# A two-layer graph, state-space and mixture kernel: earlier lists and counts, four dense steps moved into the features, the last listed sums moved into the second mixture, and the last loads split in halves

## The chip, the cores and the metric

The kernel runs on one core of one Trainium2 chip, as one program with one launch. The core has five engines that run side by side, each through its own list of instructions in order: TensorE (PE in the profile; its weight loads are PEld), VectorE (DVE), ScalarE (ACT), GpSimd (POOL) and SyncE (SP, which only issues transfers). Transfers are carried out by 16 DMA engines. The metric is the device time of one execution in microseconds, the median of several executions. No clock of the host comes into it.

## The reference

There are 4096 tokens with 256 features, and one fixed 4096x4096 matrix `adj` (about 9 nonzero entries in a row, each row divided by its number of entries). Two layers follow each other, and each adds the result of a graph block and then that of a mixture of experts:

```python
# layer 0
h = layernorm(relu(adj @ layernorm(x) @ gcn_w + gcn_b))
xz = h @ w_in                       # 256 -> 2 x 512
u  = silu(causal_conv4(xz[:, :512])); z = xz[:, 512:]
dt, B, C = projections of u         # softplus for dt
for t: state = exp(dt[t] * A) * state + dt[t] * B[t] * u[t]     # 512 x 16
       ys[t] = state @ C[t]
x1 = x + ((ys + u * D_skip) * silu(z)) @ w_out
x2 = x1 + sum over 2 of 8 experts: weight * (gelu(n @ W1) @ W2),   n = layernorm(x1)
# layer 1
f   = tanh(relu(adj)**2), of each row the 700 largest kept
h2  = tanh(layernorm(x2) @ W_proj + b_proj)
x3  = x2 + relu(f @ (h2 @ W_gcn) + b_gcn)
out = x3 + sum over 2 of 6 experts (three layers each), weights by softmax
```

A row of `adj` has far fewer than 700 positive entries, so the 700 largest are all of them. The kernel counts the positive entries of each row, and only if a count is over 700 does it run a slow second way at its end.

## The kernel before, in words

**Tiling.** Tokens go in 8 chunks of 512 (`NC`, `CW`), each of four tiles of 128. Everything is computed in float32. The span has seven stages, in this order.

1. *Start.* The graph product of layer 0 for chunk c is the generator `propagation(c)`: two halves of 256 columns, each of 32 pieces, a piece being two matrix products; every four pieces need one 512 KB tile `at` of the transposed matrix, from a ring of three buffers. With `count=True` VectorE also adds up, for each `at` tile, which entries are positive (`cnt`, lines 864 and 866; each reads the tile, so the tile's buffer is free again only after TensorE and VectorE have both read it). At the end of a half the counts are summed over partitions by TensorE and their maximum goes to `cmax`. Chunk 0 is counted here. Beside it, `lists.pair` (lines 543 to 640) makes *lists*: for chunks 2, 4 and 6 (`LISTED`) the nonzero entries of a row are found by VectorE as up to 24 positions and values. Two of the six pairs of tiles are made in this stage (`EARLY_PAIRS`, 12 steps of the generator each), the other four in stage 3. The lists of stage 1 take their buffers from the tile name `hc`.
2. *Scans.* `Front(c)` prepares a chunk (its pieces of work are placed at steps by `PLAN` and `EARLY`), then 32 steps a chunk do two scans on VectorE (line 1377), a product by C (1387), the input product on GpSimd (1354) and sums on TensorE (1404). The last work of `Front(0)` on VectorE ahead of the first scan is `do_soft` (lines 1081 to 1089), in four parts.
3. *First mixture* of layer 0, with `expert_tiles`.
4. *Features* (`features`): per chunk the mixture's result is loaded (`yg`) and combined, normalised, turned by TensorE, projected (`project`), and multiplied by W_gcn (`weigh`) into `gn`, which also goes to the DRAM tensor `gnd`.
5. *Dense steps.* For chunks 0, 1, 3, 5 and 7 the product f @ gn is done in 16 steps each, 80 in all (`seq`, counted by k): `fetch(k)` loads 512 KB of the matrix, `source(k)` turns it into f by three ScalarE activations and, except in chunk 0, adds to the chunk's count on VectorE; `product(k)` is 8 matrix products. `finish(c)` adds bias and residual. Sources run `LEAD` = 3 steps ahead, loads `AHEAD` = 2 more; three f tiles are made ahead of the features already. In the same loop the listed chunks are done by gathers (`Listed`): a *slot* is one gather of 128 rows of `gnd` by GpSimd (line 1726) into one of 12 row buffers, and one or two multiply-adds of 128x256 into x3 on VectorE (1742), 216 slots and 288 sums in all. `taken.upto(int(PACE * (k - 2)))` fixes after which step which slot is summed; a buffer that is summed is at once refilled. Four row buffers are tiles of their own (`ring`), four lie in x3 of chunk 7 and four in x3 of chunk 6 until those are written. `ROUTES` names the step at which the routing of a finished chunk begins (about 13 pieces, one a step), `TABLES` the step at which the tables of the second mixture begin.
6. *Second mixture* (`tiles1`), first the 23 tiles of chunks 0 to 4, then the 15 of chunks 5 to 7. Per tile: two gathers by GpSimd (`xk`, line 495), four turns, a copy by VectorE (`xkT`, 737), three layers, a bias add on VectorE (`yk`, 702) and two scatters by GpSimd (504). `also(n)` adds a little other work after each tile: in the first 23 the routing of chunks 7, 6, 5, later the outputs of chunks 0 to 4.
7. *End.* For chunks 5 to 7 both rows of each token are loaded, weighted, added to x3 and stored (`to_out`, `combine`): chunk 5 in whole loads of 512 KB, chunk 6 in halves, chunk 7 whole; all on the SP queue, with three `yg` buffers.

**What sets the order.** In stages 1, 2, 4 and 5 the order of each compute engine is the order in which the program text issues the work; in stages 4 and 5 that holds for SP too. Elsewhere a scheduler places instructions by its own estimate. Either way the order is fixed when the program is built: on the chip each engine takes its list in turn and waits at whatever is not ready.

Of the kernel before, what the change touches and what calls it, by code (L numbers as in the profile page):

```python
# [10 lines left out]
F32 = mybir.dt.float32  # L11
# [25 lines left out]
PACE = 2.85  # L37
ROUTES = {17: 0, 29: 2, 33: 1, 49: 3, 55: 4}
TABLES = 69
# [7 lines left out]
def kernel(ctx: ExitStack, tc: tile.TileContext, out: bass.AP, **a):  # L47
# [735 lines left out]
    with ExitStack() as s1:  # L783
# [70 lines left out]
        def propagation(c, count=False):  # L854


            halves = psts[c] = []
            for r0 in range(c * CW, c * CW + CW, HW):
                pt = ps_pt.tile([P, DB, HW], F32, name="pt", tag="pt")
                for j4 in range(NT // 4):  # L860
                    at = ats.pop(0) if ats else adjacency(r0, j4)
                    if count and j4 == 0:
                        cnt = w2p.tile([P, 4, HW], BF16, name="cnt0", tag="db")
                        nc.vector.tensor_scalar(cnt, at, 0.0, None, ALU.is_gt)
                    elif count:
                        nc.vector.scalar_tensor_tensor(cnt, at, 0.0, cnt, ALU.is_gt, ALU.add)
                    for jj in range(4):
                        j = 4 * j4 + jj
                        for k in range(DB):

                            nc.tensor.matmul(  # L871
                                pt[:, k, :], xl[:, j, k * P:(k + 1) * P], at[:, jj, :],
                                start=(j == 0 and k == 0), stop=(j == NT - 1 and k == DB - 1),
                            )
                        yield
# [3 lines left out]
                if count:  # L879
                    pc = ps_y.tile([P, CW], F32, name="psy", tag="psy")  # L880
                    for jj in range(4):
                        nc.tensor.matmul(
                            pc[:1, :HW], ones[:, :1], cnt[:, jj, :], start=(jj == 0), stop=(jj == 3)
                        )
                    h = (r0 // HW) % 2
                    nc.vector.tensor_reduce(chalf[:, h:h + 1], pc[:1, :HW], AX.X, ALU.max)
                    if h == 1:
# [527 lines left out]
        with tc.manual_schedule(engines={  # L1415
# [71 lines left out]
            for _ in range(EARLY_LISTS - NT // 4):  # L1487
                next(made)
            prop, left = propagation(1), 2 * NT + 2 - late
            for i in range(9, STEPS):  # L1490
                fr.at(i, Front.EARLY)
                fr.at(i)
                if i == 11:
                    for _ in made:
                        pass
# [3 lines left out]
            advance(left)  # L1499
            steps, tails, kept, gated, summed, owed = [], [], {}, [], 0, 0  # L1500
# [86 lines left out]
    with ExitStack() as s2:  # L1587
# [109 lines left out]
        ring += [x3[:, NT - TPC + t, :] for t in range(TPC)]  # L1697
# [7 lines left out]
        for t in ring + early_ring:  # L1705
            nc.gpsimd.memset(t, 0.0)
# [3 lines left out]
        class Listed:  # L1710
# [3 lines left out]
            def __init__(self):  # L1714
                self.slots = [(q, s) for q in range(lists.n) for s in range(PAIR)]
                self.free, self.at, self.next, self.done = early_ring + ring, {}, 0, 0
                self.last = len(self.slots) - TPC // 2 * PAIR - 12

            def fetch(self):
                if self.next >= self.last:  # L1720
                    self.free = [f for f in self.free if any(f is r for r in ring)]
# [10 lines left out]
            def upto(self, n):  # L1732
                while self.done < min(n, len(self.slots)):
# [20 lines left out]
                    self.fetch()  # L1754

# [52 lines left out]
        def features():  # L1808
# [6 lines left out]
            for c in range(1, NC):  # L1815
                if c + 1 < NC:
                    fs[c + 1].sums()
                fs[c].turn()
                fs[c - 1].weigh()
                if c + 1 < NC:  # L1820
# [21 lines left out]
        def source(k):  # L1842
# [6 lines left out]
            if c == 0:  # L1849
# [47 lines left out]
        with tc.manual_schedule(engines={  # L1897
# [8 lines left out]
            features()  # L1906
            taken.fetch()
            for k, (c, j2) in enumerate(seq):
                if k == TABLES:
# [16 lines left out]
                if k >= TABLES:  # L1926
                    next(table, None)
                taken.upto(int(PACE * (k - 2)))
                product(k, pf)
                if j2 == H2 - 1:  # L1930
                    ended = (c, pf, total(c) if c else None)
            finish(*ended)
        assert not routes and taken.done == len(taken.slots)
# [35 lines left out]
    with ExitStack() as s4:  # L1969
# [10 lines left out]
        def routing():  # L1980
            for b in range(NC - SPLIT - 1, -1, -1):
# [11 lines left out]
        def also(n):  # L1993
            if n == few[0]:
# [12 lines left out]
        for b in range(NC - SPLIT):  # L2007
            stores.append(to_out(dp1[1], b, op[0], 1 + b % 2))
# [165 lines left out]
```

## Time and profile before

| | us |
|---|---|
| median of 7 runs | 2304.73 |
| lowest and highest | 2299.45, 2309.87 |
| the profiled execution | 2303.46 |
| its span, first to last instruction | 2301.6 |
| TensorE busy in the span | 2087.7 (91%) |
| VectorE busy | 1812.5 (79%) |
| GpSimd busy | 1393.2 (61%) |
| ScalarE busy | 1195.8 (52%) |

Stage limits in the span, from the first instructions of each: start 0 to 158, scans to 1253, first mixture to 1570, features to 1672, dense steps to 2015, second mixture to 2275, end to 2301.6.

How to read it: times are microseconds from the first instruction of the span. "L1742" is line 1742 of the kernel before. A timeline line gives start, length, engine, line, operation, written tile `<-` read tiles, the number of instructions merged into it, and in brackets the idle time of that engine just before it and what ended it. In a table of stretches each engine has its busy time and, in brackets, its instructions; then the granted TensorE clock (1.00 is full speed), the busy share of the DMA engines, and what they moved.

### The profile page before, as it was taken

The page shows a single profiled execution, that of the slowest core. Times are in us where ns is not written, and L with a number is a line of the kernel's source. Part 1 is how long each engine was busy: PE and PEld are TensorE (multiplying, and loading weights), DVE is VectorE, ACT ScalarE, POOL GpSimd, SP SyncE. Part 2 cuts the span into 40 slices and gives each one's busy share as a digit, 9 for nine tenths or more (in the row PEclk, how much of TensorE's full clock was granted, in tenths as well). Part 3 has the DMA queues.
Part 4 walks back from the last instruction along what each step waited for, and adds up shares of the span by engine and source line. Part 5 has one row for each costly group of instructions (what it writes and reads, how often), then busy time and mean ns, then how long its engine had stood idle before and what let it go on. Part 6 is the DMA issues. An engine that isn't in the chain of part 4 may idle for free. (4 is left out here: it accounts for less than half of the span.)

```text
span 2301.6 us, 28092 instructions
## 1 busy us (share of the span) xinstructions
PE 2087.7 (91%) x8235; PEld 1494.1 (65%) x8235; DVE 1812.5 (79%) x3207; ACT 1195.8 (52%) x2064; POOL 1393.2 (61%) x1056
## 2 busy tenths in 40 slices
PE   7898999999999999989799799995899989899994
PEld 6665564666656566655466588783588778678773
DVE  6959999999999999999998889214448999954242
ACT  4145746566574656657675222422488677533221
POOL 1027778777777878777764445442067777856651
PEclk9999999999999999999899799997899999999997
DMA  9549999998999999899885899863265555477794
GB/s 292 175 147 260 235 274 243 257 264 229 279 243 273 247 245 270 238 270 269 236 280 175 282 329 354 254 204 126 101 190 180 177 155 175 143 236 217 241 327 157
DMA packets 302677, 532.29 MB, mean 231 GB/s; under 512 B 31323, under 2 KB 170575, under 8 KB 301616
## 3 DMA queue, kind: packets, MB, share of 16 engines
q1 hardware_dynamic: 244720, 416.84, 56.5%
q0 software_dynamic: 57792, 113.54, 22.1%
q8 instruction: 69, 1.13, 0.2%
q14 instruction: 96, 0.79, 0.1%
HBM read 434.34 MB, written 49.02 MB: 210 GB/s over the span
## 5 line engine op out<-in xcount | busy, mean ns | idle before, releaser
L1354 POOL TENSOR_TENSOR db<-du,bb 128x1024 f32<-128x1024 f32 x256 | 607.0, 2371 | 312.4 <-DVE hc L1387 74.9
L1377 DVE TENSOR_TENSOR_SCAN db<-da,state,db 128x512 f32<-128x512 f32 x512 | 627.2, 1265 | 20.4 <-ACT da L1370 18.1
L871 PE MATMUL pt<-at,gn 128*128 128x256 f32 x2048 | 479.2, 387 | 17.5 <-ACT gn L129 9.8
L871 PEld LDWEIGHTS pt<-at,gn 128*128 128x128 f32 x2048 | 396.9, 195 | 138.9 <-issue 62.7
L1370 ACT ACTIVATE da<-dt,negA 128x512 f32<-128x512 f32 x512 | 346.1, 688 | 245.4 <-DVE db L1377 235.7
L1387 DVE TENSOR_TENSOR hc<-db,cb 128x1024 f32<-128x1024 f32 x256 | 327.4, 1279 | 17.8 <-issue 0.4
L1404 PE MATMUL psy<-hc,ident 128*128 128x512 f32 x560 | 291.4, 614 | 1.9 <-DMA hc<-hc 1.9
L1864 PE MATMUL pf<-gn,f 128*128 128x256 f32 x1280 | 289.0, 387 | 0.0
L1864 PEld LDWEIGHTS pf<-gn,f 128*128 128x128 f32 x1280 | 247.1, 194 | 37.0 <-issue 3.3
L712 PE MATMUL ps_h<-xkT,wk 128*128 128x256 f32 x864 | 213.8, 390 | 13.1 <-DVE xkT L737 10.1
L697 PE MATMUL ps_y<-wk,hk 128*128 128x256 f32 x864 | 214.1, 383 | 0.2
L702 DVE TENSOR_TENSOR yk<-ps_y,bk 128x512 f32<-128x512 f32 x73 | 50.2, 688 | 204.2 <-PE ps_y L697 171.8
L1391 POOL DMA_DIRECT2D hc<-hc x232 | 201.9, 870 | 0.2
L712 PEld LDWEIGHTS ps_h<-xkT,wk 128*128 128x128 f32 x864 | 159.5, 193 | 49.0 <-DVE xkT L737 14.9
L1726 POOL DMA_INDIRECT x<-gnd,ls_idx x128 | 149.2, 1166 | 62.3 <-DMA gnd<-gn 21.7
L697 PEld LDWEIGHTS ps_y<-wk,hk 128*128 128x128 f32 x864 | 161.6, 192 | 21.8 <-ACT hk L716 1.4
L1404 PEld LDWEIGHTS psy<-hc,ident 128*128 128x128 f32 x560 | 105.2, 194 | 81.8 <-issue 59.6
L999 PE MATMUL ps_xz<-hT,w_in 128*128 128x512 f32 x256 | 117.0, 600 | 14.1 <-ACT hT L983 7.4
L1726 POOL DMA_INDIRECT ring<-gnd,ls_idx x88 | 110.1, 1251 | 31.3 <-issue 11.6
L716 ACT ACTIVATE hk<-ps_h,d0r_b 128x256 f32<-128x256 f32 x104 | 49.0, 473 | 137.5 <-PE ps_h L712 137.5
L1016 PE MATMUL ps_xz<-xc,dK 128*128 128x512 f32 x256 | 114.8, 592 | 0.0
L1846 ACT ACTIVATE f<-at 128x1024 f32<-128x1024 f32 x80 | 84.4, 1055 | 48.8 <-PE pf L1864 39.0
(398 smaller groups left out, 2998.5 us busy)
## 6 DMA issues: line engine op xcount, KB each, us to landing
at<-in_adjT_dram SPq DMA_DIRECT2D x208, 512.0 KB, 4.8
bb<-bcd SPq DMA_DIRECT2D x128, 512.0 KB, 5.3
cb<-bcd SPq DMA_DIRECT2D x128, 512.0 KB, 5.2
hc<-hc POOLq DMA_DIRECT2D x232, 256.0 KB, 5.5
wk<-in_L_ffn_W_dram SPq DMA_DIRECT2D x70, 512.0 KB, 6.2
wk<-in_L_ffn_expert_w_dram SPq DMA_DIRECT2D x114, 256.0 KB, 4.0
ls_at<-in_adj_dram SPq DMA_DIRECT2D x32, 512.0 KB, 8.5
hc<-in_adj_dram SPq DMA_DIRECT2D x16, 512.0 KB, 5.1
```

The costliest lines, as they stand in the source:

```text
L697: nc.tensor.matmul(ps[:, j, :], hT[:, m, j * P:(j + 1) * P], w[:, m, :], start=(m == 0), stop=(m == kb_out - 1),)
L712: nc.tensor.matmul(ps[:, j, :], w[:, d, m * P:(m + 1) * P], xT[:, d, :], start=(d == 0), stop=(d == DB - 1),)
L871: nc.tensor.matmul(pt[:, k, :], xl[:, j, k * P:(k + 1) * P], at[:, jj, :], start=(j == 0 and k == 0), stop=(j == NT - 1 and k == DB - 1),)
L999: nc.tensor.matmul(ps, w_in[:, k, m * P:(m + 1) * P], self.hT[:, k, :], start=(k == 0), stop=(k == DB - 1),)
L1354: nc.gpsimd.tensor_tensor(self.db, self.f.du[self.half][:, self.mi:self.mi + 1, :].to_broadcast([P, 2, CW]), self.bb, ALU.mult,)
L1370: nc.scalar.activation(da, self.f.dt[self.half][:, self.mi, :], AF.Exp, scale=negA[:, self.m, n:n + 1])
L1377: nc.vector.tensor_tensor_scan(self.db[:, j, :], da, self.db[:, j, :], state[:, self.m, n:n + 1], ALU.mult, ALU.add,)
L1387: nc.vector.tensor_tensor(self.hc, self.db, self.cb, ALU.mult)
L1391: nc.gpsimd.dma_start(self.hc[:, 0, :], self.hc[:, 1, :], accum_op=ALU.add)
L1404: nc.tensor.matmul(f.psy[m], ident, self.hc[:, j, :], start=False, stop=(self.g == GS - 1 and j == last),)
L1726: nc.gpsimd.indirect_dma_start(out=to[:, :], out_offset=None, in_=gnd[:, :], in_offset=bass.IndirectOffsetOnAxis(ap=lists.idx[:, q, s:s + ...
L1864: nc.tensor.matmul(pf[:, t, :], f[:, jj, t * P:(t + 1) * P], gn[:, j, :], start=(j == 0 and t % 2 == 0), stop=(j == NT - 1 and t % 2 == 1),)
```

## The change

- **Start.** The 12 list steps stay in the loop of chunk 0 only as far as 8; the other 4 of the first pair and all 12 of the second no longer stand ahead of `Front(0)`'s VectorE work, but are spread behind it, from step 11 on. Chunk 1 is now counted in `propagation(1, True)` as well (16 `cnt` instructions, the buffers taken from the names `du` and `dt`, one sum of both halves in the bank of `pt`), and no longer in the dense loop.
- **Features.** The steps k = 0 to 3 (`FIRST1`) of the dense product are done inside `features`, one in each of the rounds c = 2 to 5, ahead of the turn; the source and load that go with a step follow `weigh`. The dense loop begins at k = 4, and its slots go by `2.8 * (k - 6)`. `ROUTES` and `TABLES` move with it; the last tables come two pieces a step.
- **Listed sums.** Twelve slots are left when the dense loop ends. They use only the four buffers of `ring` (from the fourth last step on, `narrow`), and `also` takes two slots after each tile (`SPARE`). The late routing takes chunk 5, then 7, then 6, since chunk 6 is the listed one that is finished last.
- **End.** All twelve half loads of chunks 5 to 7 (256 KB each) are issued at once, one of each pair on SP and one on ScalarE's queue, into twelve buffers of the tile pool; sums and stores go by halves, the stores alternately on both queues.

```diff
-PACE = 2.85
-ROUTES = {17: 0, 29: 2, 33: 1, 49: 3, 55: 4}
-TABLES = 69
+PACE = 2.8
+SPARE = 2
+FIRST1 = 4
+ROUTES = {17: 0, 33: 2, 35: 1, 49: 3, 59: 4}
+TABLES = 72
...
                     if count and j4 == 0:
-                        cnt = w2p.tile([P, 4, HW], BF16, name="cnt0", tag="db")
+                        h = (r0 // HW) % 2
+                        tag = {"tag": "db"} if c == 0 else {"tag": ("du", "dt")[h], "bufs": 3}
+                        cnt = w2p.tile([P, 4, HW], BF16, name="cnt0", **tag)
+                        cnts.append(cnt)
...
-            for _ in range(EARLY_LISTS - NT // 4):
-                next(made)
-            prop, left = propagation(1), 2 * NT + 2 - late
+            prop, left = propagation(1, True), 2 * NT + 2 - late
             for i in range(9, STEPS):
                 fr.at(i, Front.EARLY)
                 fr.at(i)
                 if i == 11:
-                    for _ in made:
-                        pass
+                    next(made)
+                elif i > 11:
+                    for _ in range(2 if i < 14 else 1):
+                        next(made, None)
...
-                self.free, self.at, self.next, self.done = early_ring + ring, {}, 0, 0
+                self.free, self.at, self.next, self.done = early_ring + late_ring + ring, {}, 0, 0
+                self.kept = ring + late_ring
...
+            def narrow(self):
+                self.kept = ring
+
+            def lent(self):
+                return [g for g, f in self.at.items() if any(f is r for r in late_ring)]
...
             for c in range(1, NC):
                 if c + 1 < NC:
                     fs[c + 1].sums()
+                k = c - 2
+                if 0 <= k < FIRST1:
+                    product(k, pf)
                 fs[c].turn()
                 fs[c - 1].weigh()
+                if 0 <= k < FIRST1:
+                    source(k + LEAD)
+                    fetch(k + LEAD + AHEAD)
                 if c + 1 < NC:
                     fs[c + 1].norm()
                 fs[c].project()
...
-            if c == 0:
+            if c < 2:
                 pass
...
             for k, (c, j2) in enumerate(seq):
+                if k < FIRST1:
+                    continue
...
                 if k >= TABLES:
-                    next(table, None)
-                taken.upto(int(PACE * (k - 2)))
+                    for _ in range(1 if k < TABLES + 4 else 2):
+                        next(table, None)
+                if k == len(seq) - 4:
+                    taken.narrow()
+                taken.upto(int(PACE * (k - FIRST1 - 2)))
+                if k == len(seq) - 1:
+                    taken.upto(max(taken.lent(), default=0) + 1)
                 product(k, pf)
...
-            for b in range(NC - SPLIT - 1, -1, -1):
+            for b in (0, 2, 1):
...
         def also(n):
+            taken.upto(taken.done + SPARE)
...
-        for b in range(NC - SPLIT):
-            stores.append(to_out(dp1[1], b, op[0], 1 + b % 2))
+        d = dp1[1]
+        halves = [(b, h) for b in range(NC - SPLIT) for h in range(2)]
+        tags = [("wk0", 3), ("wk1", 3), ("wk2", 3), ("xk", 4)]
+        homes = [tag for n in range(4) for tag in tags if n < tag[1]]
+        pairs, queues = [], [nc.sync, nc.scalar]
+        for b, h in halves:
+            pair = []
+            for i in range(2):
+                tag, bufs = homes.pop(0)
+                t = tp.tile([P, 2, D], F32, name="yl", tag=tag, bufs=bufs)
+                r0 = (i * d.S + b) * CW
+                rows = d.ys[r0:r0 + CW, :].rearrange("(p t) d -> p t d", t=TPC)
+                ld = queues[i].dma_start(t, rows[:, 2 * h:2 * h + 2, :])
+                for o in d.sent[-4:]:
+                    after(ld, o)
+                pair.append(t)
+            pairs.append(pair)
+        for (b, h), pair in zip(halves, pairs):
+            o = op[0].tile([P, 2, D], F32, name="ol", tag=("oc", "yg")[b % 2], bufs=2 + b % 2)
...
+            stores[c].append(
+                queues[(b + h) % 2].dma_start(tokens(out, c)[:, 2 * h:2 * h + 2, :], o)
+            )
```

## The prediction, made before the changed kernel had run

> **What bounds the kernel now.** I read the page, then busy time by stage, then the timelines at the four places that the change touches. By stage:
>
> ```profile
> core 0: us, PE busy (x) PEld busy (x) DVE busy (x) ACT busy (x) POOL busy (x), PEclk, DMA share, GB/s
> 80.00:120.00 40.00, 32.71 (x104) 20.34 (x103) 36.66 (x130) 10.16 (x17) 1.01 (x1) 0.87 0.35 119
> 120.00:158.00 38.00, 37.33 (x143) 25.79 (x143) 10.69 (x21) 19.05 (x24) 3.27 (x2) 1.00 0.48 152
> 158.00:470.00 312.00, 298.31 (x988) 187.26 (x987) 300.37 (x270) 185.94 (x325) 239.21 (x149) 0.97 0.94 252
> ...
> 1570.00:1672.00 102.00, 77.32 (x256) 50.08 (x257) 49.37 (x156) 40.68 (x75) 11.68 (x22) 0.83 0.35 119
> 1672.00:1730.00 58.00, 58.00 (x271) 51.05 (x270) 25.48 (x52) 53.52 (x52) 41.24 (x39) 1.00 0.68 210
> 1730.00:1850.00 120.00, 108.82 (x487) 90.39 (x485) 108.98 (x285) 89.72 (x94) 95.61 (x81) 0.96 0.58 174
> ...
> 2050.00:2180.00 130.00, 129.62 (x643) 104.95 (x642) 52.53 (x185) 44.53 (x96) 79.28 (x81) 1.00 0.74 223
> ```
>
> The start (to 158) is TensorE's, with a hole. The scans are VectorE's (96% busy; up to 1250 it waits only for ScalarE's decays). The features leave TensorE idle for 25 of 102 us. The dense steps are TensorE's for 58 us, then nobody's alone: VectorE 91%, and GpSimd 80% plus 0.30 us of issue at each gather. The second mixture is TensorE's. From the timelines of the engines, in order of time (start, length, engine):
>
> ```profile
> 85.48 1.28 DVE L948 TENSOR_TENSOR h<-ps_gcn,gcn_b 128x512 f32<-128x512 f32 x2
> 91.41 2.80 PE L976 MATMUL ps_turn<-ident,h 128*128 128x128 f32 x8 [7.23 <-ACT h L968]
> 145.52 2.36 DVE L1081 SCALAR_TENSOR_TENSOR t<-t,du 128x1024 f32<-128x1024 f32 x2 [24.02 <-ACT t L1071]
> ...
> 1656.33 2.80 PE L144 MATMUL ps_tr<-ident,xn 128*128 128x128 f32 x8 [4.08 <-ACT xn L129]
> 1976.58 0.82 PE L417 MATMUL pf<-tb_eq,d_lo 128*128 128x100 bf16 x8 [9.12 <-ACT tb_eq L429]
> 1991.68 2.90 POOL L1726 DMA_INDIRECT ring<-gnd,ls_idx  x1 [0.30 <-issue]
> 2008.67 0.97 POOL L495 DMA_INDIRECT xk<-d1a_xd,d1ap_src  x1 [0.30 <-issue]
> 2030.33 0.68 DVE L702 TENSOR_TENSOR yk<-ps_y,bk 128x512 f32<-128x512 f32 x1
> 2295.08 0.37 SPq L1964 DMA_DIRECT2D out_dram<-oc  x1
> ```
>
> The reader is to see: lists hold `h` back to 85.48 and TensorE idles 7.23; VectorE then has 24.02 us to spare before `do_soft`; late in the dense steps TensorE waits for VectorE; gathers for the second mixture start only when the listed ones end.
>
> **Start: +4.4.** `h` moves up behind the maximum, 77.05 instead of 85.48, so the turn follows the previous product at 84.18 (-7.2), and the cold matmuls after the hole (turn 2.80 where 1.04 is usual) go too. Replaying TensorE's list with the trace's lengths, the second half of `propagation(1)` starts near 135 (was 144.58). But the counts of thirteen tiles now stand ahead of `do_soft`. The last is of the fifth tile of that half, and its buffer is free after the second: 135 + 2 x 3.5 = 142, + 3.75 to land (134.92 to 138.65 in the trace), + 1.2 to count (row of line 866) = 146.9. `do_soft` starts 1.4 later than 145.52 and loses the 0.95 us in which it waited for its logarithm: scans start +0.4. The other three counts and one maximum (0.4) lie between scans, on the bounding engine: 3 x 1.2 + 0.4 = 4.0. TensorE's 9.7 us lead buys nothing. TensorE's sum of chunk 1's counts waits for the last count, some five steps in; behind it stand the sums of `hc`, whose six buffers cover 6 x 3.6 us: 0, up to 2 without that cover. On SP two more `at` loads stand ahead of the third `bb` load, which had no buffer before 160.27 anyway: 0. Bounds: -4 (all tiles in time, scans 8 earlier) to +9 (each of the last four loads takes 5.6, as the one at 140.48 did). I take the replay.
>
> **Features: +2.4.** Four steps of 16 matmul records, 3.45 us each. In rounds 3 and 5 a step fills the hole before the turn (3.71 and 3.56) and keeps the clock up: those rounds ran 10.5 and 11.4 us from turn to turn where an unbroken one runs 7.9. So 13.8 us cost about 1.5. ScalarE's source (3 x 1.06) goes into its 5.3 to 6.2 us waits in rounds 2 and 4; in rounds 3 and 5 it delays the next norm by 3.2, which product 2 covers in round 4 and nothing does in round 6. The last load of 512 KB stands ahead of chunk 7's `yg` loads on SP: 0.45 issue + 1.6 transfer, straight into the 4.08 wait at 1656.33, about +2.4 in all with the later store. Bounds 0 and +14 (nothing hidden).
>
> **Dense steps: -18.4 at the last `finish`, the features' +2.4 included.** It started at 2013.43. After: features end at 1674.5; 12 steps x 3.45 to k = 16, and 1 for VectorE: 1717. Next 16: 55.2, routing on TensorE 4.8 (line 144, 197, 673, 285 rows), 3 of waiting: 1780. TensorE sets this, as chunk 1 has no counts: VectorE's list holds 42 us there (was 61). Gathers: 45 slots at 1.06 + 0.30 (mean without counts beside) = 61, just enough. The last 48 steps: I summed VectorE's list between the finishes, each row at its line's median spacing: 189.2 before, in 209.4 elapsed; 198.4 after (chunk 2's routing moves in, twelve sums out). With the same 20 idle: 218; by gathers alone, 134 x 1.53 (busy 215.7 + 175 x 0.30 over 175 slots) = 205. I take 215: 1995. Bounds -10 and -24. The clean-up at k = 76 to 79 (`narrow`, two table pieces a step) is in the list's sum; the later `ROUTES` and `TABLES` too.
>
> **Second mixture's first tiles: +13.3.** Not free. The built order of GpSimd puts the last twelve gathers among the first fourteen `xk` gathers, and VectorE must do all twelve sums before the first `yk`. From `finish` (F) on: slot 204's gather starts at F - 2.9, since its buffer is freed by the sums just ahead of `finish`; 26 gathers x 1.27 (0.97 + 0.30) put the last at F + 29, landed 3.3 later (`ring` 2.6 to 4.1, `xk` 3.5), sum, residual, `yk` at F + 34, the copy `xkT` of the fourth tile at F + 36.5. Before, that copy was at 2035.77 and its layer at 2037.15, F + 23.7; now F + 37. TensorE has work for the first three tiles (17.8 us) and none after; later it is full (129.62 of 130), so nothing is won back. Queued behind the waiting sums: `xkT`, `yk`, chunks 5 to 7's routing; behind the gathers: the scatters. Bounds: +3 (only the two listed gathers ahead of the second `xk`) and +25 (each gather 1.7, the row at 2015.07). The other order of late routing costs 0: as many pieces, under the same tiles; the twelve memsets of row buffers stay twelve.
>
> **End: -4.6.** Loads start at 2276.5 as before. 3 MB at the 371 GB/s seen between 2278 and 2280 take 8.5 us, so VectorE sets it: first pair lands at 2279.5 (256 KB took 2.6 to 3.1 at 1569.66), 24 sums x 0.44 = 10.6: 2290.1; last store 2.6 (0.37 + 3.2 for twice the bytes before): 2292.7 instead of 2298.30, -5.6. At 250 GB/s it is 2295, -3.3. I take -4.6. The Trainium skill ("DMA: Bandwidth & Descriptors", Rules for kernel authors) says that spreading DMAs over issuing engines gives no bandwidth and saves issue time only; on that count alone this part would give six issues of 0.43, 2.6 us, an estimate, and the sum would be 2301.4 instead of 2299.4. The trace has one queue at 0.98 of the DMA engines from 2278 to 2280, as the page has it, but also 0.05 and 0.02 from 2292 to 2296, which is what an early issue fills.
>
> **Sum.** 4.4 - 18.4 + 13.3 - 4.6 = -5.3 on the profiled execution's 2303.46, that is 2298.2; that run lies 1.27 under the median shown, so 2299.4.
>
> **Rivals.**
> - *The twelve sums are hidden.* For: VectorE is busy 52.53 of 130 there. Against: the order is fixed and has them ahead of `yk`. At its bound, +3: 2289.
> - *They cost more than the dense steps gain.* One mechanism: VectorE waits for a gather ahead of a copy, GpSimd waits for that sum's buffer, three rounds of four, beside the burst of weight loads (an `xk` took 5.58 there). Above 18.6 the kernel is slower; at 25: 2299.4 + 11.7 = 2311.
> - *The features do not hide the steps* (the change only moves them): 13.8 instead of 2.4, so 2299.4 + 11.4 = 2311. Against: the holes are in the rows.
> - *The start gains.* If the counts' tiles are in time, scans start 4 earlier net: 2291.
>
> **How the numbers follow.** Chances: forecast 0.45, hidden sums 0.18, costly sums 0.17, unhidden steps 0.08, gaining start 0.12. A measurement tells about 0.2% (4.6 us) from no change: 2300.1 to 2309.3. The forecast is split by it: 0.22 faster, 0.21 same, 0.02 slower; hidden sums and gaining start give 0.28 faster and 0.02 same; costly sums and unhidden steps 0.22 slower and 0.03 same. So faster 0.50, same 0.26, slower 0.24. Range 2287 to 2311; the forecast alone 2294 to 2305.
>
> **What would show it.** Right: no 7 us wait before layer 0's first turn, yet the first scan near 158; no counts of chunk 1 after 1700; dense `finish` near 1995 + 4; a TensorE hole of 8 us or more before the fourth tile of the second mixture, ended by VectorE; last store near 2292 less the shift. Wrong: scans well before 155 or after 162, a `finish` moved by under 10, no such hole, or an end still over 24 us long.

## The result, and the profile after: slower by 0.86%

The changed kernel took 2325.66 us (median of 18 runs, 2322.07 to 2334.12), the kernel before beside it 2305.91 (46 runs): a ratio of 1.0086, with a 95% interval of 1.0077 to 1.0096. It is 20 us slower, where 5 us faster was forecast, and outside the range. The profiled execution has a span of 2323.5 us, 22.0 longer than that of before. By stage, in us, from the two profiles:

| stage | before | after | difference | forecast |
|---|---|---|---|---|
| start, to the first scan | 158.0 | 158.7 | +0.7 | +0.4 |
| scans, to the end of the last | 1088.9 | 1098.0 | +9.1 | +4.0 |
| first mixture, to the features' first load | 322.8 | 322.9 | +0.1 | 0 |
| features, first load to the last `weigh` | 102.6 | 103.4 | +0.9 | +2.4 |
| dense steps, to the last `finish` | 341.2 | 330.7 | -10.5 | -20.8 |
| last `finish` to the fourth `xkT` | 22.3 | 42.2 | +19.8 | +13.3 |
| rest of the second mixture, to the last scatter's end | 239.2 | 242.5 | +3.3 | 0 |
| from there to the end | 26.6 | 25.2 | -1.4 | -4.6 |

(The forecast's -18.4 at the last `finish` is split here into +2.4 and -20.8. The scans of the twelve profiles here in which they hold no counts took 1088.7 to 1092.4 us, so some 4 us of scatter lie in such a difference.) The busy time by stretch, as it was shown of before, each stretch at the same place in its stage:

```profile
core 0: us, PE busy (x) PEld busy (x) DVE busy (x) ACT busy (x) POOL busy (x), PEclk, DMA share, GB/s
80.00:120.00 40.00, 39.08 (x129) 22.62 (x127) 37.07 (x114) 10.19 (x17) 1.01 (x1) 1.00 0.42 131
120.00:159.00 39.00, 38.32 (x163) 30.45 (x163) 24.10 (x55) 17.78 (x22) 3.55 (x2) 1.00 0.52 164
159.00:471.00 312.00, 286.40 (x913) 175.25 (x912) 297.54 (x269) 179.74 (x317) 235.37 (x146) 0.95 0.91 241
1580.00:1683.00 103.00, 85.52 (x321) 58.21 (x322) 49.46 (x155) 52.94 (x87) 11.59 (x21) 0.90 0.41 138
1683.00:1741.00 58.00, 58.00 (x274) 51.11 (x274) 30.70 (x78) 53.76 (x52) 41.17 (x40) 1.00 0.69 212
1741.00:1861.00 120.00, 113.77 (x526) 96.58 (x525) 96.31 (x272) 96.76 (x102) 96.21 (x79) 0.97 0.58 178
2072.00:2202.00 130.00, 129.54 (x644) 105.22 (x643) 52.65 (x185) 44.60 (x96) 79.58 (x81) 1.00 0.73 223
```

TensorE's hole at the start is closed (39.08 of 40, before 32.71) and its idle time in the features falls by a third (85.52 busy of 103, before 77.32 of 102): the change does what it says. Two engines carry the loss: VectorE in the scans' first stretch is busy 297.54 instead of 300.37 though it has three counts more, so it waits longer; and TensorE idles between the dense steps and the second mixture. The timelines of the engines of the changed kernel show both, in order of time (start, length, engine):

```profile
76.42 1.27 DVE L961 TENSOR_TENSOR h<-ps_gcn,gcn_b 128x512 f32<-128x512 f32 x2
83.39 1.19 PE L989 MATMUL ps_turn<-ident,h 128*128 128x128 f32 x8
...
146.07 1.23 DVE L871 SCALAR_TENSOR_TENSOR cnt<-at,cnt 128x1024 bf16<-128x1024 f32 x1 [2.41 <-DMA at<-in_adjT_dram]
147.21 2.35 DVE L1094 SCALAR_TENSOR_TENSOR t<-t,du 128x1024 f32<-128x1024 f32 x2
158.69 2.46 DVE L1390 TENSOR_TENSOR_SCAN db<-da,state,db 128x512 f32<-128x512 f32 x2 [2.24 <-POOL db L1367]
183.52 6.05 PE L1012 MATMUL ps_xz<-hT,w_in 128*128 128x512 f32 x8 [6.04 <-ACT zs L1025]
192.83 1.03 PE L891 MATMUL pc<-cnt,ones_b 128*1 128x256 bf16 x8 [0.67 <-ACT pts L882]
193.90 0.68 DVE L896 TENSOR_REDUCE cmax<-pc 1x1 f32<-1x512 f32 x1 [6.25 <-PE pc L891]
...
2011.03 2.99 POOL L1741 DMA_INDIRECT ring<-gnd,ls_idx  x1 [8.89 <-DMA wk<-in_L_ffn_expert_w_dram]
2013.66 1.27 DVE L1909 TENSOR_TENSOR x<-pf,b_gcn_b 128x512 f32<-128x512 f32 x2
2045.71 1.01 POOL L1741 DMA_INDIRECT ring<-gnd,ls_idx  x1 [0.30 <-issue]
2048.53 0.48 DVE L1757 SCALAR_TENSOR_TENSOR x<-ring,ls_val,x 128x256 f32<-128x256 f32 x1 [0.75 <-DMA ring<-gnd,ls_idx]
2049.94 0.68 DVE L704 TENSOR_TENSOR yk<-ps_y,bk 128x512 f32<-128x512 f32 x1
2055.84 0.68 DVE L739 COPY xkT<-ps_xt 128x512 f32<-128x512 f32 x1
2056.58 2.07 PE L714 MATMUL ps_h<-xkT,wk 128*128 128x256 f32 x4 [11.39 <-DVE xkT L739]
...
2313.64 0.88 DVE L2068 SCALAR_TENSOR_TENSOR ol<-yl,d1b_wv,x 128x256 f32<-128x256 f32 x2 [2.86 <-DMA out_dram<-ol]
```

Four readings: the turn is 8 us earlier, but `do_soft` (147.21) now follows the last count's load; VectorE stands 6.25 us at the new maximum, since TensorE's sum of the counts stands behind a product that waits 6.04 us for ScalarE's `zs` copies, and then itself waits for ScalarE's `pts`; the last listed gather starts at 2045.71, and TensorE waits 11.39 us for a copy that VectorE makes behind the twelve sums; the end has a new wait, for a store. (At 2011.03 the bracket names a weight load, which can't free a row buffer; what fits is one of VectorE's sums on a row buffer, from 2009.90 on.) What the page does not show so plainly is the dense steps. All gathers of the listed chunks in the two kernels, from the groups of GpSimd's instructions (busy time, mean ns of one):

```profile
L1726 POOL DMA_INDIRECT x<-gnd,ls_idx x128 | 149.2, 1166 | 62.3 <-DMA gnd<-gn 21.7 <-DVE x L1742 11.9 <-issue 11.9
L1726 POOL DMA_INDIRECT ring<-gnd,ls_idx x88 | 110.1, 1251 | 31.3 <-issue 11.6 <-DVE x L1742 11.5 <-DVE cnt L1856 2.1
```

```profile
L1741 POOL DMA_INDIRECT x<-gnd,ls_idx x124 | 150.1, 1210 | 59.3 <-DMA gnd<-gn 20.7 <-DVE x L1757 12.4 <-issue 11.9
L1741 POOL DMA_INDIRECT ring<-gnd,ls_idx x92 | 115.7, 1258 | 36.6 <-issue 9.8 <-DMA wk<-in_L_ffn_expert_w_dram 8.9 <-DVE x L1757 5.5
```

Before, 149.2 + 110.1 = 259.3 us busy and 215 x 0.30 of issue make 323.8, and from the first gather's start (1677.2) to the last one's end (2008.4) there are 331.2: GpSimd had 7 us of room in the dense steps. Its 80% in the table by stage was busy time without the issue.

### The profile page after: what moved, and what is told of

It is laid out like the page before. It is cut to its first block, busy times and chain, and to the rows that moved or that the text cites. A ratio compares the mean times of both kernels' runs of the same rounds, so it can differ in the third digit from the quotient of the medians.

```text
span 2323.5 us, 28127 instructions
## 1 busy us (share of the span) xinstructions
PE 2085.6 (90%) x8241; PEld 1493.2 (64%) x8241; DVE 1810.9 (78%) x3207; ACT 1195.6 (51%) x2064; POOL 1401.8 (60%) x1056
## 5 line engine op out<-in xcount | busy, mean ns | idle before, releaser
L1390 DVE TENSOR_TENSOR_SCAN db<-da,state,db 128x512 f32<-128x512 f32 x512 | 627.1, 1265 | 18.4 <-ACT da L1383 16.2
L1741 POOL DMA_INDIRECT ring<-gnd,ls_idx x92 | 115.7, 1258 | 36.6 <-issue 9.8
L718 ACT ACTIVATE hk<-ps_h,d1ap_b 128x256 f32<-128x256 f32 x92 | 43.4, 473 | 133.8 <-PE ps_h L714 133.8
```

What stands on the lines that cost most here:

```text
L1390: nc.vector.tensor_tensor_scan(self.db[:, j, :], da, self.db[:, j, :], state[:, self.m, n:n + 1], ALU.mult, ALU.add,)
L1741: nc.gpsimd.indirect_dma_start(out=to[:, :], out_offset=None, in_=gnd[:, :], in_offset=bass.IndirectOffsetOnAxis(ap=lists.idx[:, q, s:s + ...
```

## The experiments

The ratios are to runs of the kernel before on the same chip. The chips differ: the kernel before took 2360 us in the first set (u) and 2376 in the second (v0 to v3 and `v1_combined`), 2305 and 2310 in the third (`v1_again` and w) and fourth (x), about as on the prediction's chip. The changed kernel itself ran on the prediction's chip alone, so a difference to it compares two ratios, or two profiles, from two chips. So whole times are judged by the last two sets, and from the first two only stages away from the dense steps are used. u and x are edits of the changed kernel, v2 and v3 of the kernel before, v1 and w combinations.

**Chunk 1's counts** (u1, x2): counted in the dense loop again, with the early list order kept.

```diff
-            prop, left = propagation(1, True), 2 * NT + 2 - late
+            prop, left = propagation(1), 2 * NT + 2 - late
...
-            if c < 2:
+            if c == 0:
...
-                    ended = (c, pf, total(c) if c > 1 else None)
+                    ended = (c, pf, total(c) if c else None)
```

> The changed kernel with chunk 1's counts back in the dense loop (early list order kept). In the profiles the changed kernel is 9.1 us behind at the end of the scans (0.7 of it at their start) and 22.0 behind at the end of the span. Theory (the counts cost the start and the scans: do_soft stands behind them on VectorE, three counts and one waiting maximum lie between scans): do_soft starts with the turn, 8 us earlier than before, so the first scan is near 150 instead of 158.7, the last scan ends near 1239 instead of 1256.7; the dense loop gives back 16 x 1.2 us of VectorE, of which about 5 us show; the whole comes out 5 to 10 us above the kernel before. Rival 1 (the start is set by TensorE's second half of the product and its loads, not by the counts): first scan stays near 158, last scan near 1248, the whole 11 to 16 above before. Rival 2 (VectorE in the dense loop has no room): scans as in the theory, but the last finish moves by more than 15 against the start of the dense steps, and the whole stays 15 or more above before.

> The changed kernel with chunk 1's counts back in the dense loop, once more. By the stages of the first set: first scan 9.9 us earlier than in the changed kernel, the scans 5 to 6 us shorter, the dense steps 5 to 8 us longer. Theory (the counts cost the start and the scans about 15 us and save the dense steps about 6): 7 to 12 us faster than the changed kernel, so a ratio of 1.0034 to 1.0056 to before. Rival (the counts cost the dense steps as much as they save the scans): within 4 us of the changed kernel, 1.007 to 1.010.

Measured: u1 0.9947 (0.9926 to 0.9968) on its chip; x2 1.0060 (1.0042 to 1.0079), 6 us less than the changed kernel, between the theory's 7 or more and the rival's 4 or less. (u1's whole time came out below the kernel before on that chip, and not 5 to 10 us above it.) In x2 the first scan comes at 148.2, the scans take 1091.7, the dense steps 7.5 us more than in the changed kernel (338.2 against 330.7, `weigh` to `finish`). From x2's timeline of VectorE:

```profile
135.73 2.36 DVE L1094 SCALAR_TENSOR_TENSOR t<-t,du 128x1024 f32<-128x1024 f32 x2 [13.76 <-ACT t L1084]
148.18 2.46 DVE L1390 TENSOR_TENSOR_SCAN db<-da,state,db 128x512 f32<-128x512 f32 x2 [2.24 <-POOL db L1367]
```

`do_soft` starts 11.5 us earlier and waits for ScalarE alone. So the counts cost the start 10.5 us and the scans 6.3, and save 7.5 later. The stages are the theory's; of the sum the profiles show 10.6 us and the medians 6.0 with some 4 either way, so its size is left between 4 and 10.

**The waiting maximum** (u2, x4): only the maximum moves.

```diff
+                    def most(n=n, h=h, pc=pc):
+                        nc.vector.tensor_reduce(
...
+                        due.append(most)
...
                 cur.product()
+                if n == 8:
+                    due.pop()()
```

> The changed kernel with one instruction moved: VectorE's maximum of chunk 1's counts is issued after step 8's products, one to two steps later in VectorE's order; TensorE's sums of the counts stay where they are. In the changed kernel this maximum waited 6.25 us for TensorE. Theory (VectorE's scans stood behind that wait): the wait is gone, the last scan ends about 6 us earlier than in the changed kernel (near 1251), and the whole is 13 to 15 us above before instead of 20. Rival (TensorE and ScalarE are late there anyway, and the wait only shows a delay that the scans would meet next): the last scan stays within 2 us of 1256.7 and the whole 18 to 21 above before.

> The changed kernel with the maximum of chunk 1's counts one to two steps later in VectorE's order, once more. In the first set the scans took 1093.6 us with it, against 1097.1 and 1097.5 of two kernels without it. Theory (the wait of 6.25 us is partly taken up by the next wait for TensorE): the scans take 1092 to 1095 where the changed kernel's took 1098.0, the whole 3 to 5 us faster than the changed kernel. Rival (all of it counts): 6 or more.

Measured: u2 1.0076 (1.0043 to 1.0110), x4 1.0083 (1.0064 to 1.0102). The scans took 1093.6 and 1093.7 us instead of the 1097.0 to 1098.0 of four kernels without the edit. From x4's timeline of VectorE:

```profile
194.68 2.46 DVE L1395 TENSOR_TENSOR_SCAN db<-da,state,db 128x512 f32<-128x512 f32 x2 [2.63 <-ACT da L1388]
198.74 0.67 DVE L897 TENSOR_REDUCE cmax<-pc 1x1 f32<-1x512 f32 x1
200.62 2.46 DVE L1395 TENSOR_TENSOR_SCAN db<-da,state,db 128x512 f32<-128x512 f32 x2 [1.20 <-ACT da L1388]
```

The maximum waits for nothing now, but of its 6.25 us some 4 are won: the next scans wait 2.63 and 1.20 for ScalarE's decays. The first of these stands in ScalarE's order behind the copy `pts`, which waits 2.00 us for TensorE (193.40); the second stands behind a 1.91 us activation of `zs` and two table loads of 1.28 us (195.31 to 199.82). In the whole time (0.7 us less than the changed kernel's ratio, some 4 either way) 4 us can't be told from none.

**The twelve late sums** (u3, x3): all slots in the dense loop.

```diff
-PACE = 2.8
+PACE = 2.96
...
-                if k == len(seq) - 4:
-                    taken.narrow()
...
-            taken.upto(taken.done + SPARE)
```

> The changed kernel with all 216 listed slots summed inside the dense loop (2.96 slots a step instead of 2.8; nothing left for the second mixture, no narrowing to four row buffers). From the last finish to the fourth xkT copy the kernel before took 22.3 us and the changed one 42.1. Theory (the twelve late sums stand ahead of the first yk and xkT copies on VectorE, and their gathers among the first xk gathers on GpSimd): that stretch is back at 22 to 25; GpSimd's 216 gathers at 1.53 us each end the dense steps near 1688 + 331 + 5 = 2024 instead of 2013.7, so the net is 8 to 12 us: the whole 8 to 12 above before. Rival 1 (GpSimd is not the bound of the dense steps): finish stays near 2014 and the whole is at or under 2 above before. Rival 2 (the stretch is long for another reason, the late routing's other order): it stays over 35 and the whole is 25 or more above before.

> The changed kernel with all listed slots in the dense loop, once more. Theory (from the last finish to the fourth xkT copy 20 to 23 us instead of 42; the chain of gathers, 12 longer at 1.6 us and without its 8.9 us of idle time, ends the dense steps 10 us later): 8 to 13 us faster than the changed kernel, 1.003 to 1.005 to before. Rival (the twelve gathers cost the dense steps as much as the second mixture): within 4 us of the changed kernel.

Measured: u3 1.0032 (1.0004 to 1.0060) on its chip; x3 1.0047 (1.0028 to 1.0066), 9 us less than the changed kernel, as the theory has it. From x3's timeline:

```profile
2029.00 1.27 DVE L1909 TENSOR_TENSOR x<-pf,b_gcn_b 128x512 f32<-128x512 f32 x2
2050.66 0.69 DVE L739 COPY xkT<-ps_xt 128x512 f32<-128x512 f32 x1 [0.28 <-PE ps_xt L735]
```

The handover takes 21.7 us again, and the dense steps 15 more than with the twelve left out (346.0 against 330.7).

**The end** (u4; v3 is the new end, in place, on the kernel before).

```diff
-            o = op[0].tile([P, 2, D], F32, name="ol", tag=("oc", "yg")[b % 2], bufs=2 + b % 2)
+            o = x3[:, c * TPC + 2 * h:c * TPC + 2 * h + 2, :]
```

> The changed kernel with the last outputs summed in place in x3 instead of in output buffers, so that chunk 7's sums need not wait for chunk 5's stores. In the changed kernel VectorE waited 2.86 us there (2310.8 to 2313.6), and the last put to the end of the span took 25.2 us. Theory (that wait sets the end): 2.5 to 3.5 us off, the end takes 22 to 23. Rival (the DMA engines, busy 0.9 and more from 2301 to 2314, set the end): under 1 us off.

> The kernel before with the new end alone, and with the sums in place in x3 (no output buffers): twelve half loads issued at once on two queues. Theory (order of loads on one queue, three row buffers and late stores made the end long): last put to end of span 22 to 22.5 us instead of 26.6, the whole 4 to 5 us faster. Rival (the DMA engines' rate sets it): 1 to 2 us faster.

Measured: u4 1.0092 (1.0064 to 1.0120), v3 1.0003 (0.9990 to 1.0016). In the profiles the end after the last scatter takes 21.7 and 21.1 us, where the changed kernel needs 25.2 and the kernel before 26.6: 3.5 and 5.5 off, about as both theories have it for the stage. The whole times do not show it: v3's theory had 4 to 5 us, and none are measured (its second mixture was 2 us longer). So this part rests on the stage. From u4's timeline:

```profile
2355.13 6.29 SPq L2056 DMA_DIRECT2D yl<-d1b_ys  x6
2355.20 7.06 ACTq L2056 DMA_DIRECT2D yl<-d1b_ys  x6
2361.05 8.18 DVE L2068 SCALAR_TENSOR_TENSOR x<-yl,d1b_wv,x 128x256 f32<-128x256 f32 x20 [1.13 <-DMA yl<-d1b_ys]
```

The sums run through (20 in 8.18 us), with no wait for a store.

**The list order alone, the combination, and the kernel before on the second set's chip** (v2, v1, v0). v2 has of the change only the moved `next(made)`; v1 is the changed kernel with the edits of u1, u3 and u4 together.

> The kernel before, unchanged, for a profile on the chip that the other kernels of this set run on. Expected: ratio 1.000. The first set's chip took 2360 us for it, 54 more than the first one; the changed kernel's dense steps took 36 us more there (368 instead of 331) and its second mixture 6 more. If the chip is what differs, this profile shows the same excess in the same two stages.

> The kernel before with the early list order alone (4 list steps ahead of the first chunk's VectorE work, the other 12 steps spread behind it); chunk 1's counts stay in the dense loop. Theory (the lists held the first turn back, and nothing else binds the start): the first scan comes 8 to 9 us earlier, every later stage is shifted by as much, the whole 7 to 9 us faster. Rival (the scans' other conditions, TensorE's second half of the product, ScalarE's decays, take the lead back): under 3 us faster.

> The changed kernel with chunk 1's counts back in the dense loop, all listed slots in the dense loop, and the last sums in place: what stays of the change is the early list order, the four dense steps in the features and the new end. Theory 1 (the three repairs act on separate stages and add up, by the runs of the first set: 12 us under before with the first repair, 23 less with the second, 3 less with the third): 34 to 40 us faster than before. Theory 2 (GpSimd's 216 gathers of 1.53 us, which start when the features end, bound the dense steps, so that moving four steps into the features gains next to nothing there): 9 of the lists, 5 of the end and 0 to 4 of the rest, 12 to 18 us faster.

> The combined kernel of the second set once more (early list order, four dense steps in the features, all counts and all listed slots in the dense loop, last sums in place), as the base of this set. Expected: 0.6 to 1.0% faster than before. From the first gather to the end of the last one 216 gathers take 340 to 380 us, whatever the four moved steps free on TensorE.

Measured: v0 1.0000; v2 0.9983 (0.9962 to 1.0004), its first scan 9.0 us earlier than v0's and the lead whole at the end of the scans (1242.4 against 1251.5); in the whole time 4 us are measured, less than the theory's 7 to 9, and the interval reaches no change. v1 took 0.9907 (0.9891 to 0.9924) there, 22 us less, between its two theories, and, once more, 0.9984 (0.9973 to 0.9995) on a chip like the first, where it had been expected 0.6 to 1.0% under the kernel before. By these last ratios the repairs take 23.5 us off the changed kernel (1.0086 to 0.9984), and 18.5 by the single ones: 6.0, 9.0 and the end's 3.5. v0 shows what is particular to the second set's chip:

```profile
ACT f L1846 <- remote: 34.1, 2, 28.8
PEld pf L1864 <- issue: 32.9, 21, 2.7
PE pf L1864 <- issue: 25.1, 20, 2.2
```

Beside the first gathers ScalarE stands once for 28.8 us, and in the same 28.8 us TensorE starts one product only every 1.4 to 2.8 us, although it waits for nothing that the profile names ("issue"), while the gathers go on. To k = 16 the dense steps took 94 us instead of 60. What held the two engines up is not shown: a late load of the matrix would explain ScalarE's wait, but not TensorE's pace.

**Who bounds the dense steps** (w2, w1, w3, all against v1 on one chip). w2 puts the four steps back (`FIRST1 = 0`, with before's `PACE`, `ROUTES` and `TABLES`). w1 makes the dense loop's counts with one input on VectorE and adds them up on TensorE; w3 does the listed sums, but for the first of each row, on 64 of 256 columns:

```diff
-                nc.vector.scalar_tensor_tensor(cnt, at, 0.0, cnt, ALU.is_gt, ALU.add)
+                nc.vector.tensor_scalar(cnt, at, 0.0, None, ALU.is_gt)
...
+                    nc.tensor.matmul(
+                        pcs[c][:1], ones[:, :1], cnt[:, jj, :], start=(j == 0), stop=(j == NT - 1)
+                    )
```

```diff
+                            w = slice(0, D if first else 64)
                             nc.vector.scalar_tensor_tensor(
-                                acc, buf, lists.val[:, 2 * q + h, n_:n_ + 1],
-                                b_gcn_b if first else acc, ALU.mult, ALU.add,
+                                acc[:, w], buf[:, w], lists.val[:, 2 * q + h, n_:n_ + 1],
+                                b_gcn_b if first else acc[:, w], ALU.mult, ALU.add,
                             )
```

> The combined kernel with the four dense steps back in the dense loop (80 steps there, pace and routing steps as before). Theory (the chain of gathers starts when the features end and sets the end of the dense steps, so the moved steps bought nothing): within 5 us of the combined kernel. Rival (the prediction: the steps are worth their 13.8 us of TensorE less 2.4): 8 to 14 us slower than the combined kernel.

> The combined kernel with the counts of the dense loop made differently: VectorE only marks the positive entries (one input, 0.75 us by the row of the first piece of a chunk, instead of a two-input multiply-add of 1.22), and TensorE adds the marks up, two small products a step. In the kernel before a gather beside the 1.22 us form took 1.44 us, beside the marking form 1.18, with no count beside it 1.04. Theory (GpSimd's chain of gathers bounds the dense steps, and the two-input counts stretch it): gathers beside counts near 1.1, the chain 25 to 35 us shorter; TensorE pays about 0.45 x 64 = 29 us and becomes the next limit, so 10 to 20 us faster than the combined kernel. Rival 1 (TensorE has no room): 5 to 15 slower than the combined kernel. Rival 2 (the counts are not what stretches the gathers): they stay at 1.4 to 1.6 and the chain as long as it was.

> The combined kernel with all but the first multiply-add of each listed row done on 64 of 256 columns only; the other columns are left out, so the output is not the reference's. VectorE loses some 264 x 0.25 = 65 us of work in the dense steps, with the same instructions, waits and gathers. Theory (GpSimd's gathers bound the dense steps): the chain of gathers and the last finish come within 8 us of the combined kernel's. Rival (VectorE bounds them, as the prediction had it: 91% busy): 30 us or more earlier.

Measured: v1 0.9984, w2 0.9970 (0.9952 to 0.9988), w1 0.9934 (0.9912 to 0.9956), w3 2281.02 us in one run (its output is not the reference's, since columns are left out). The dense steps took 351.3 (v1), 347.5 (w2), 341.0 (w1) and 331.9 us (w3); first to last gather 339.5, 335.9, 327.0 and 318.8. The gathers of v1, then of w1, then of w3:

```profile
L1741 POOL DMA_INDIRECT x<-gnd,ls_idx x132 | 165.6, 1254 | 62.8 <-DMA gnd<-gn 19.2 <-issue 14.9 <-DVE x L1757 13.7
L1741 POOL DMA_INDIRECT ring<-gnd,ls_idx x84 | 104.7, 1247 | 25.6 <-issue 8.5 <-DVE x L1757 6.7 <-DVE cnt L1883 1.5
```

```profile
L1741 POOL DMA_INDIRECT x<-gnd,ls_idx x132 | 156.0, 1182 | 71.5 <-DVE x L1757 22.6 <-DMA gnd<-gn 20.8 <-issue 15.2
L1741 POOL DMA_INDIRECT ring<-gnd,ls_idx x84 | 94.7, 1127 | 25.6 <-issue 9.8 <-DVE x L1757 7.3 <-DMA x<-gnd,ls_idx 1.2
```

```profile
L1741 POOL DMA_INDIRECT x<-gnd,ls_idx x132 | 154.5, 1170 | 62.5 <-DMA gnd<-gn 20.9 <-issue 16.2 <-DVE x L1758 9.6
L1741 POOL DMA_INDIRECT ring<-gnd,ls_idx x84 | 97.2, 1157 | 25.6 <-issue 11.9 <-DVE x L1758 6.1 <-DMA x<-gnd,ls_idx 2.4
```

w2: the four steps bought nothing; to the `finish` at k = 16 v1 is 13.6 us ahead, and it gives all of it back. w3 lies between its theories: VectorE sheds some 55 us and then waits for gathers, which is most of what the waits of w3 show:

```profile
DVE x L1758 <- DMA x<-gnd,ls_idx: 66.7, 32, 25.1
DVE x L1758 <- DMA ring<-gnd,ls_idx: 27.5, 24, 3.7
```

What it gains, 19.4 us, is about what the gathers themselves became shorter: 216 x (1.251 - 1.165) = 18.6. Gathers and issue fill 317 of the 318.8 us from w3's first gather to its last. So GpSimd bounds, and VectorE's two-input instructions lengthen its gathers. (How much of the 18.6 is theirs is less sure: between v1 and w2, which have the same sums and counts, the mean gather differs by 0.05 us too, and w3 ran once.) w1 shortens them as well (beside a count 1.33 us instead of 1.53, not the 1.1 expected; its chain of gathers is 12.5 us shorter, not 25 to 35), and then meets TensorE, which is full for three stretches between `finish` and `finish`:

```profile
1712.00:1782.00 70.00, 70.00 (x310) 51.01 (x309) 53.20 (x142) 53.50 (x55) 55.37 (x49) 1.00 0.60 184
1782.00:1858.00 76.00, 76.00 (x343) 55.08 (x342) 64.78 (x198) 55.48 (x60) 59.94 (x53) 1.00 0.55 165
1858.00:1933.00 75.00, 75.00 (x335) 54.55 (x335) 60.05 (x173) 54.86 (x58) 52.94 (x42) 1.00 0.52 160
```

**The best of it** (x1: w1 with the four steps back).

> Early list order and the new end with sums in place, the counts of the dense loop marked by VectorE with one input and added up by TensorE, all 80 dense steps and all listed slots in the dense loop. In the last set the same with four steps in the features was 0.66% faster than before, and taking those four steps back (with the two-input counts) was worth 3.5 us. Theory (the two add up): 0.7 to 0.9% faster than before. Rival (with shorter gathers TensorE bounds the dense steps, and the four steps would have been worth their 11 us there): 0.2 to 0.5% faster.

Measured: 0.9941 (0.9920 to 0.9962), between the two theories and not to be told from w1; each is 0.6 to 0.7% faster than before, the best on these chips of the kernels that compute the whole output. The dense steps took 346.4 us, 5.3 more than w1's, and the features 3.1 less: with TensorE as the bound the four moved steps are worth something again, but not their 13.8 us.

## Why the prediction was wrong, step by step

- **Start, +4.4: measured +9.8.** The replay was right: `do_soft` at 146.9 (147.21), first scan +0.4 (+0.7). What failed is the sentence that TensorE's sum of the counts costs "0, up to 2": it looked for buffers behind the sum on TensorE, and not at the maximum, which stands in VectorE's order between two scans and is done by the same sum. It waited 6.25 us; x4 shows some 4 of them as the maximum's own, and the other 5 to 6 are near the forecast's 4.4, given the scatter of the scans. The step also asked only what the counts cost, and took it that TensorE's lead "buys nothing": x2 shows that without the counts 10 us of it reach the scans.
- **Features, +2.4: measured +0.9.** Right in kind: 13.8 us of TensorE's work made the stage 0.9 us longer.
- **Dense steps, -20.8 from the features' end: measured -10.5.** To k = 16 it was 41.5 us (42.4 forecast), the next sixteen steps 64.3 (63). The step that failed is "I take 215" for the last 48, between VectorE's 218 and the gathers' 205: it took GpSimd's bound for the lower, slack one. These steps took 224.9. The 132 gathers that begin in them took 1.32 us and 0.30 of issue each, not 1.53 together, which is 214, and `narrow` left GpSimd 8.9 us without a buffer (not tried by itself). The forecast's price was a mean over the last 175 gathers; in the last 48 steps a gather beside a two-input count took 1.62 us, in the kernel before 1.49, and why it grew is open. (VectorE's list was also summed too short: it was busy 196 of the 209.4 us, not 189.2.) The gain of 10.5 is not that of the four steps, which w2 shows to be nothing; taken alone, the twelve slots that were left out are worth 15 by x3 and chunk 1's counts 7.5 by x2. These do not simply add up, nor is the base the same on each chip: w2, with nearly the dense loop of before, took 347.5 and not 341.2. The profile had it: 324 of 331 us of GpSimd were gathers and their issue.
- **Second mixture's first tiles, +13.3: measured +19.8.** The mechanism was right, and this is where most of the loss is. Two sizes were off. The 26 gathers ran without a gap, as forecast, but took 1.37 us each, issue and the first one's 2.99 included, and ended at F + 33 instead of F + 29; `yk` followed at F + 36.3 (F + 34). Then VectorE did 5 us of chunks 5 to 7's routing and of flags between `yk` and the fourth copy, at F + 42.2 (F + 36.5). "TensorE is later full, so nothing is won back" held, and 3.3 more were lost: 1.8 up to the sixth copy and 1.5 at one later tile. The rival "they cost more than the dense steps gain" was the true case (19.8 against the 10.5 of the dense steps; the forecast had put the point from which it decides at 18.6). Half of its mechanism was: VectorE waited for gathers ahead of the copies, but GpSimd waited for no buffer after `finish`.
- **End, -4.6: measured -1.4.** The first pair landed 3.0 us after its issue, as forecast, and the sums run through where nothing else holds them (u4); the loads are slower than the forecast's 8.5 us (their last landing shown is 12.4 us after the first issue), but after the second pair no sum waits for them. The working forgot the output buffers: chunk 7's sums wait 2.86 us for chunk 5's stores, which stand behind the loads on both queues and among them on the DMA engines. u4 removes it, and with its 3.5 the end is as forecast (-4.9). The rule weighed there is not contradicted: in no slice of 0.6 us of the end did the DMA engines move more than 413 GB/s after, 410 before; the gain is an earlier start, not a higher rate.
- **The sum.** -5.3 was forecast and +22.0 measured; the 27 us between are 5.4 at the start, 10.3 of the dense steps less 1.5 of the features, 9.8 in the second mixture and 3.2 at the end. All errors but that of the features have one sign. In three of them an instruction's place in an engine's order was read as free (the maximum, the copies behind the routing, the sums behind the stores); in the dense steps an engine without room was read as slack.

## What to carry to other kernels

Add an engine's issue time to its busy time before calling another engine the bound: GpSimd's 80% were 98%. Work taken off a full engine (TensorE here) gains nothing where another chain starts at a fixed event and is as long; ask when that chain starts and how long it is. And a small instruction, such as a maximum of one number, that waits in the order of the bounding engine costs its wait (some 4 of 6.25 us here) and not its length of 0.7: put it where its input is long ready.

## What the runs showed of the hardware

- In the kernel before, a gather by GpSimd took 1.04 us on average with no count beside it and 1.44 beside VectorE's 1.22 us count of two inputs (1.61 in the changed kernel, single ones up to 3.2). Beside the one-input form of 0.75 us it took 1.18 in six cases there, 1.33 in w1's 83 and 1.19 in x1's 91. The Trainium skill ("SBUF — State Buffer", Who interferes with whom) says that a VectorE instruction with two SBUF inputs contends with a GpSimd instruction that reads SBUF. The runs agree so far as shorter two-input instructions (w3, 0.29 instead of 0.48 us) and one-input ones (w1) both came with shorter gathers.
- Loads issued "all at once" did not go out at once: in the changed kernel each of the two queues issued four loads of 256 KB within some 1.5 us (SP 2299.87 to 2301.26), SP's fifth at 2302.88, when its first had landed at 2302.86, and ScalarE's sixth at 2306.67, when its second had landed at 2306.65. x1 shows the same (SP's fifth at 2273.41, its first landed at 2273.40). That four outstanding loads are a queue's limit was not tried by itself.
- The same kernel took 2305 to 2310 us on the prediction's chip and on those of the third and fourth set, and 2360 and 2376 on the other two. On one of these (v0) the first sixteen dense steps took 34 us longer; in 28.8 us of them ScalarE stood still and TensorE ran slowly, with the DMA engines moving only some 50 GB/s. Why was not tried.
